# Two products of batch 1 moved between batch 0's tiles of scores, one value step put ahead of the fourth burst, and two kinds of setup matmuls cut into four

## The chip, the cores and the metric

The kernel runs on one core of a Trainium2 chip. The metric is the time of one execution on the device in microseconds (us), as the median of several runs; lower is better. The engines of the core are TensorE (PE in the profile, its weight loads PEld), VectorE (DVE), ScalarE (ACT), GpSimd (POOL) and SyncE (SP), which here only issues DMAs.

## The reference

A graph attention layer over 16 batches of 512 nodes with 512 features. A node may attend to the first 20 nodes only (the "keys"), in two directions d, with 16 heads of 32 features. The code is cut to what matters, with sizes for some symbols.

```python
row_zero = exp_v.sum(-1) == 0
q_exp = jnp.where(row_zero[..., None], 0.0, q[:, None, :])
self_feat = concatenate([exp_v, q_exp], axis=-1) @ W_self.T + b_self
output = self_feat
for d in range(2):
    A = adj_f if d == 0 else jnp.swapaxes(adj_f, 1, 2)
    A = A[:, :, :20, :]
    cond, vb = A.sum(-1), A @ w_bias + b_bias
    kv = self_feat[:, :20]
    qh = (self_feat @ Wq[d].T + bq[d]).reshape(B, N, 16, 32)
    kh = (kv @ Wk[d].T + bk[d]).reshape(B, 20, 16, 32)
    aff = einsum('bnhd,bmhd->bnhm', qh, kh) / sqrt(32)
    aff = where(cond[:, :, None, :] > 0, aff, NEG) + vb[:, :, None, :]
    w = softmax(aff, axis=-1)
    out_t = einsum('bnhm,bmf->bnhf', w, kv)
    output = output + einsum('bnhf,hgf->bnhg', out_t, Wout[d]) + bout[d]
return exp_v + relu(output)
```

## The kernel before

All matrices are float32. The kernel folds the query weights into the keys (so that scores are products of `self_feat` with a prepared matrix `g` per batch) and the output weights into the values. It has a setup and then a loop over the 16 batches.

**Order.** The order of instructions on every engine is the order in which the program text issues them (`manual_schedule`); waits between engines follow from the data. Tiles come from pools with few buffers, and a new tile in a buffer waits for the last use of the old one. In the loop the matmul banks of products and attention are four fixed ones (`bank(name, 0)` to `bank(name, 3)`, tag `acc0` to `acc3`); scores use pairs of banks from `ps_s`, two pairs in turn.

**The forms of a matmul.** Most matmuls are cut into four along their outputs: `for a in range(HL)` with R = 32 outputs each, so that four of them write the four quarters of a bank's partitions. In the profile such a group has the shape "128\*32", an uncut one "128\*128". Each float32 matmul shows as two records of PE and two of PEld.

**Setup** (lines 458 to 786). `kv_terms` (line 537) multiplies the first 20 nodes of all batches (`xkv`, 320 columns) with the self weights `ws_v`, in four steps k of the contraction and four banks fc; between steps stand the projection of the query condition (`ps_q`, lines 548 and 560) and the sum over `rsk` (line 555), which flags rows that are zero. `key_rows` (line 589) makes the projected keys `khD`, with VectorE copying them out of the bank (line 602). Then come 20 "bursts" (`keys`, line 672): each makes a part of `g`, with matmuls of the shape "32\*128", read by ScalarE (line 696) and VectorE (line 698). Between bursts PE does other work, so that the banks of a burst can be read: the rest of the key rows for the first four, and then what the list `plan` (line 726) names per burst, one letter per step:

- `v` and `w`: `values` (line 645), four (or eight) matmuls of the values with 512 columns; the fourth step of a tile copies it out on VectorE (line 660) and sends it off by DMAs issued on GpSimd (line 664). One `v` step stands ahead of the burst itself where n is 4 (line 749).
- `n`: `row_flags` (line 211), one matmul of a matrix of ones with the row sums, which gives the zero-row flags of batch 0 or 1.
- `p`: one of the seven products of batch 0 (below), with the VectorE step that reads it.
- `m`, `b`, `c`: bias terms.

Burst n in the program counts from 0; the text counts from one, so that the fourth burst is n = 3.

**Products.** The self features of nodes 20 to 511 are made in the way of a fast 2x2 block multiplication, with seven products per batch (`product(b, n)`, line 250) of 16 matmuls each, 246 columns wide. Products 1, 6, 7 and 4 add in turn onto the same two banks `ps_a` (acc0 and acc1), product 2 has `ps_d` (acc2), products 5 and 3 share `ps_c` (acc3). VectorE reads the banks between them: `partial` (line 285, L289) reads `ps_a` after products 1, 6, 7 and 4, two instructions each time; `joined` (line 297, L299) adds `ps_d` or `ps_c`. So product 6 must not start before the `partial` that follows product 1 has read `ps_a`.

**The loop.** Each batch b has four tiles nt of 128 nodes. A tile's `scores` (line 349) are 64 matmuls; `weigh` (line 376) then adds the mask, takes the maximum and subtracts it on VectorE (L379, L383, L387), `expo` takes the exponential on ScalarE (L392), `normal` (L415 to L417) divides by the sum, `turn` (L424) transposes the weights, and `attend` (L435) multiplies them with the values of the batch, once per batch, in tile 2 of the batch after. The products of batch b + 1 run within batch b: 1 and 2 behind the scores of tile 2, 6 ahead of the scores of tile 3, 7 and 5 behind them; 4 and 3 run in the next batch's tile 0. `weigh` of tile 2 takes a function `between` that puts `partial(b + 1, 0, 0)` on VectorE between the maximum and the subtraction. The masks go through `mask_mul` (ScalarE, L317), `mask_sum` (VectorE, L328), `mask_spread` (ScalarE, L337) and `full_add` (GpSimd, L344).

Around the change the PE order of batch 0 is: scores of tiles 0, 1 and 2; products 1, 2 and 6 of batch 1; scores of tile 3; products 7, 5 and 4; then tile 0 of batch 1, product 3, tile 1, the attention of batch 0.

Of the kernel before, what the change touches and what calls it, by code (L numbers as in the profile page):

```python
# [13 lines left out]
P = 128  # L14
# [4 lines left out]
def gat_kernel(  # L19
# [20 lines left out]
    nc = tc.nc  # L40
    B, F, N = xT.shape
    NG, L = adj.shape[3], adj.shape[4]
    H, DH = 16, 32
    C = F // P
    HL = P // DH
    NT = N // P
    BM = B * NG
# [4 lines left out]
    R = P // HL  # L52
# [20 lines left out]
    ws_v = const.tile([P, C, F], F32, name="ws_v")  # L73
# [137 lines left out]
    def row_flags(b):  # L211
        ps = bank(f"ps_nz{b}")
        nc.tensor.matmul(ps[:, :N], ones, rss[b], start=True, stop=True)  # L213
        nzs[b] = load.tile([P, N], F32, tag="nz", name=f"nz{b}")
        nc.vector.tensor_scalar(nzs[b], ps[:, :N], 0.0, None, ALU.not_equal)
# [109 lines left out]
    def mask_sum(b, h):  # L325

        add = conds[b, h] = msk.tile([P, 2 * S], F32, tag="add", name=f"add{b}_{h}")
        done["masks"] = nc.vector.tensor_reduce(add, prods.pop((b, h)), AX.X, ALU.add)  # L328
        adds[b, h] = msk.tile([P, 2, HL, S], F32, tag="both", name=f"both{b}_{h}")
# [128 lines left out]
    with tc.tile_pool(name="setup", bufs=1) as sp, tc.tile_pool(name="ps_acc", bufs=4, space=PSUM) as acc["pool"]:  # L458
# [12 lines left out]
        ones = sp.tile([P, P], F32, name="ones")  # L471
# [6 lines left out]
        with tc.tile_pool(name="setup_k", bufs=1) as sk:  # L478
# [58 lines left out]
            def kv_terms(fc, k):  # L537
                nc.tensor.matmul(  # L538
                    kv_ps[fc][:, :BM], ws_v[:, k, bass.ts(fc, P)], xkv[:, k],
                    start=(k == 0), stop=(k == C - 1),  # L540
                )

# [80 lines left out]
        with tc.tile_pool(name="setup_g", bufs=4) as sg:  # L623
# [101 lines left out]
            }  # L725
            plan = "mmvv bvv vvc vvc vvn vvw vvw vw wn p p p p p p p".split()

# [17 lines left out]
            for n, runs in enumerate(bursts):  # L745
                for i in range(len(rest)):
                    if (i < 1 and n > 0) or any(fc == 0 and (d, hg) == rest[0] for fc, hg, d, _, _ in runs):
                        key_rows(*rest.pop(0))
                if n == 4:
                    values(*steps["v"].pop(0)[1])  # L750
# [44 lines left out]
    with tc.manual_schedule():  # L795
# [10 lines left out]
        for b in range(B):  # L806
# [7 lines left out]
            for nt in range(NT):  # L814
# [13 lines left out]
                if nt == 0:  # L828
                    if b == 0:
                        for g in range(2):  # L830
                            scores(b, nt, g, ps[g])
                        mask_sum(b, 1)
                    else:
# [48 lines left out]
                if nt == 1:  # L882
# [11 lines left out]
                    for g in range(2):  # L894
                        scores(b, nt, g, ps[g])
                    if last:
                        for c in (0, 1):
                            nc.scalar.activation(biased[:, c], sfs[b][:, c], AF.Identity, bias=bo[:, c : c + 1])
# [17 lines left out]
                if nt == 2:  # L916
# [27 lines left out]
                    if more:  # L944
                        product(b + 1, 1)
                        product(b + 1, 2)
                        new_self(b + 1)
# [69 lines left out]
        b = B - 1  # L1017
# [77 lines left out]
```

## Time and profile before

| what | value |
|---|---|
| time, three runs | 582.24, 582.80 and 580.28 us; median 582.24 us |
| the profiled execution | 581.09 us, its span (first to last instruction) 579.3 us |
| mean granted clock of TensorE | 0.998 |
| PE busy | 572.1 us |
| DVE, POOL, ACT busy | 492.8, 405.5, 393.8 us |
| DMA | 123.26 MB, mean 213 GB/s |
| scores, the costliest group (L365) | 8192 records, 277.4 us |
| products (L283) | 3584 records of six groups, 29.6 to 59.4 us each |

All durations come from that one profiled execution. Its span begins with the first instruction; the rest of its 581.09 us lies around the span. A row of the timeline gives the start, the duration, the engine, the line, the operation with its tiles, the shape of the operands and the number of records (x); in brackets stands the idle time of the engine before it and what ended it. "issue" there means that the engine waited for nothing that the profile shows. A row of the windows view gives for each stretch its length and then, for PE, PEld, DVE, ACT and POOL, the busy time and the records, and at last the granted clock of PE, the mean busy share of the DMA engines and the rate in GB/s.

### The profile page before, as it was taken

The numbers are of one execution on the slowest core, as the hardware profiler recorded it, in microseconds if no ns is written. First come the engines' busy times: TensorE is split into PE (matmuls) and PEld (weight loads), VectorE is DVE, ScalarE is ACT, GpSimd is POOL, SyncE is SP. The second block draws the span as 40 slices with busy tenths as digits, with TensorE's granted clock in tenths as the row PEclk, the third lists the DMA queues.
The fourth block names the chain that finished last, engine by engine and source line by source line (L and its number), as shares of the span: only waits on it lengthen the run. The fifth ranks groups of instructions, "written<-read, shape, count | busy, mean of one in ns | idle before, by whom it ended". The sixth has DMA issues, their size and how long they took to land.

```text
span 579.3 us, 30986 instructions
## 1 busy us (share of the span) xinstructions
PE 572.1 (99%) x13496; PEld 434.0 (75%) x13496; DVE 492.8 (85%) x790; ACT 393.8 (68%) x1162; POOL 405.5 (70%) x383
## 2 busy tenths in 40 slices
PE   9999999999999999999999999999999999999996
PEld 6544458888878787878778787887887878787873
DVE  0685676979898989898999999898989898989896
ACT  1234554587878777778786868687887877777571
POOL 2636977648686776858585867786858677786874
PEclk9999999999999999999999999999999999999999
DMA  8999998757776777778576767576666766664404
GB/s 287 386 405 311 335 363 290 210 144 220 210 233 183 207 203 201 215 178 235 169 217 168 219 168 209 165 216 179 203 197 188 202 195 182 194 202 111 146 19 147
DMA packets 98787, 123.26 MB, mean 213 GB/s; under 512 B 18876, under 2 KB 66968, under 8 KB 96604
## 3 DMA queue, kind: packets, MB, share of 16 engines
q1 hardware_dynamic: 96124, 117.80, 66.2%
q0 software_dynamic: 1392, 2.43, 1.8%
q8 instruction: 106, 1.74, 1.3%
q10 hardware_dynamic: 1136, 1.06, 0.5%
q14 instruction: 29, 0.24, 0.1%
HBM read 82.30 MB, written 40.24 MB: 212 GB/s over the span
## 4 chain that ended last, share of the span: by engine, by line
PE 97%; DMA 1%; DVE 0%; issue 0%; SPq 0%; DVEq 0%
PE ps_s L365 46%; PE ps_a L283 19%; PE ps_c L283 9%; PE ps_o L435 6%; PE ps_d L283 5%; PE ps_v L654 3%; PE ps_k L596 3%; DMA ws_q<-in_wsT 1%; PE ps_o L798 1%; PE ps_kv L538 0%; PE ps_nz L213 0%; PE ps_s L354 0%; PE _g(0, 2, 0, 14, 16)0_440 L681 0%; PE _g(2, 2, 0, 14, 16)0_836 L681 0%; PE _g(1, 2, 0, 14, 16)0_644 L681 0%
## 5 line engine op out<-in xcount | busy, mean ns | idle before, releaser
L365 PEld LDWEIGHTS ps_s<-g,sf 128*32 128x32 f32 x8192 | 263.1, 110 | 21.8 <-issue 14.7
L365 PE MATMUL ps_s<-g,sf 128*32 128x152 f32 x8192 | 277.4, 293 | 0.7 <-issue 0.7
L337 ACT COPY both<-add 32x80 f32<-32x80 f32 x512 | 130.9, 256 | 61.0 <-DVE add L328 55.1
L417 POOL TENSOR_TENSOR s<-s,sm 128x640 f32<-128x640 f32 x63 | 80.4, 1276 | 96.0 <-DVE sm L416 73.5
L344 POOL TENSOR_TENSOR full<-cq,both 128x640 f32<-128x640 f32 x64 | 100.4, 1569 | 26.8 <-issue 20.9
L317 ACT ACTIVATE prod<-adj,wb_sb 128x80 f32<-128x80 int32 x330 | 112.4, 431 | 0.0
L392 ACT ACTIVATE s<-s 128x640 f32<-128x640 f32 x63 | 46.5, 738 | 55.4 <-DVE s L387 55.0
L449 POOL TENSOR_TENSOR o<-o,x 128x512 f32<-128x512 f32 x60 | 76.3, 1293 | 0.0
L379 DVE TENSOR_TENSOR full<-ps_s,full 128x608 f32<-128x608 f32 x63 | 48.7, 773 | 21.6 <-PE ps_s L365 19.0
L415 DVE TENSOR_REDUCE sm<-s 128x32 f32<-128x640 f32 x63 | 50.8, 806 | 10.7 <-ACT s L392 10.5
L283 PE MATMUL ps_a<-t,ws_s 128*32 128x246 f32 x1024 | 59.4, 371 | 0.0
L383 DVE TENSOR_REDUCE ps_s<-full 128x32 f32<-128x640 f32 x63 | 52.2, 828 | 2.2
L424 DVE STREAM_TRANSPOSE wt<-s 128x640 f32<-128x640 f32 x63 | 52.7, 837 | 0.6 <-POOL s L417 0.6
L387 DVE TENSOR_TENSOR s<-full,ps_s 128x640 f32<-128x640 f32 x63 | 51.5, 817 | 1.1
L289 DVE SCALAR_TENSOR_TENSOR sf<-nz,qw,ps_a 128x246 f32<-128x246 f32 x128 | 51.5, 442 | 0.2
L283 PEld LDWEIGHTS ps_a<-t,ws_s 128*32 128x32 f32 x1024 | 34.2, 110 | 16.7 <-issue 0.6
L328 DVE TENSOR_REDUCE add<-prod 128x80 f32<-128x960 f32 x32 | 36.8, 1149 | 7.2 <-ACT prod L317 7.2
L446 ACT ACTIVATE o<-o,bo 128x512 f32<-128x512 f32 x60 | 38.3, 710 | 0.6 <-DVE o L444 0.6
L248 POOL TENSOR_TENSOR t<-x,t 128x492 f32<-128x492 f32 x32 | 36.8, 1151 | 1.3
L248 POOL TENSOR_TENSOR t<-x 128x492 f32<-128x492 f32 x32 | 36.9, 1154 | 0.0
L435 PE MATMUL ps_o<-wt,vd 32*32 32x512 f32 (+5 forms) x816 | 36.8, 578 | 0.1
L444 DVE TENSOR_TENSOR o<-ps_o,sf 128x512 f32<-128x512 f32 x60 | 36.7, 668 | 0.0
(225 smaller groups left out, 715.4 us busy)
## 6 DMA issues: line engine op xcount, KB each, us to landing
g<-g_d SPq DMA_DIRECT2D x60, 304.0 KB
g_d<-st SPq DMA_DIRECT2D x16, 1064.0 KB
out_T<-o SPq DMA_DIRECT2D x60, 256.0 KB
xn<-in_xn SPq DMA_DIRECT2D x56, 256.0 KB
x<-in_xT SPq DMA_DIRECT2D x56, 256.0 KB
adj<-in_adj SPq DMA_DIRECT2D x60, 220.0 KB
nz<-nz_d SPq DMA_DIRECT2D x14, 256.0 KB
wk<-in_wkT SPq DMA_DIRECT2D x2, 1024.0 KB
```

The source lines that it names most:

```text
L248: done["xsum"] = nc.gpsimd.tensor_sub(t, one, two)
L283: nc.tensor.matmul(to, lhs, x[:, k], start=start, stop=stop, skip_group_check=n != 2)
L289: done["partial"] = nc.vector.scalar_tensor_tensor(to[:, i], nzs[b][:, half(l)], qw[:, 2 * f + i, b : b + 1], parts[b, "a"][i][:, :HN], AL ...
L317: nc.scalar.activation(p[:, :, l], a[:, :, l], AF.Identity, scale=wb_sb[:, l : l + 1])
L337: done["spread"] = nc.scalar.copy(adds[b, h][bass.ts(a, R), :, g], add[r].rearrange("p (t m) -> p t m", t=2))
L344: done["full"] = nc.gpsimd.tensor_add(f, cqs[b].unsqueeze(1).to_broadcast(shape), adds[b, nt // 2][:, nt % 2].unsqueeze(2).to_broadcast(sh ...
L365: nc.tensor.matmul(to, sfs[b][:, k, bass.ds(nt * P + (2 * g + j) * R, R)], of, start=(onto is None and k == 0 and (whole or j == 0)), stop ...
L383: nc.vector.tensor_reduce(mx, f, AX.X, ALU.max)
L417: done["normal"] = nc.gpsimd.tensor_mul(s, s, sm.unsqueeze(3).to_broadcast(full))
L424: nc.vector.transpose(wts[b][:, nt], s.rearrange("p a h m -> p (a h m)"))
L435: nc.tensor.matmul(banks[a][bass.ds(at // 2 * DH, n * DH)].rearrange("p (t n) -> p t n", n=32), vd[r, bass.ds(at * DH, n * DH)], wt[r, :, ...
L449: nc.gpsimd.tensor_add(o[:, c], o[:, c], xs[b][:, c])
```

## The change

- Products 1 and 2 of batch 1 no longer stand behind batch 0's third tile of scores (nt = 2): product 1 stands behind its first tile, product 2 behind its second. Other batches are as before. VectorE's order in the loop is the same; the `partial` that follows product 1 stays inside `weigh` of tile 2.
- One value step stands ahead of burst n = 3 as well as n = 4. As the number of steps is fixed, the seventh entry of `plan` (behind burst n = 10) has one `v` fewer. Three copies of value tiles on VectorE (L660) thereby come ahead of the evacuation of the next burst, and their DMAs on GpSimd's queue move with them.
- `row_flags` and `kv_terms` are cut into four matmuls of 32 outputs each, over the same columns.

```diff
     def row_flags(b):
         ps = bank(f"ps_nz{b}")
-        nc.tensor.matmul(ps[:, :N], ones, rss[b], start=True, stop=True)
+        for a in range(HL):
+            nc.tensor.matmul(ps[bass.ts(a, R), :N], ones[:, :R], rss[b], start=True, stop=True)
...
             def kv_terms(fc, k):
-                nc.tensor.matmul(
-                    kv_ps[fc][:, :BM], ws_v[:, k, bass.ts(fc, P)], xkv[:, k],
-                    start=(k == 0), stop=(k == C - 1),
-                )
+                for a in range(HL):
+                    nc.tensor.matmul(
+                        kv_ps[fc][bass.ts(a, R), :BM], ws_v[:, k, bass.ds(fc * P + a * R, R)], xkv[:, k],
+                        start=(k == 0), stop=(k == C - 1),
+                    )
...
-            plan = "mmvv bvv vvc vvc vvn vvw vvw vw wn p p p p p p p".split()
+            plan = "mmvv bvv vvc vvc vvn vvw vw vw wn p p p p p p p".split()
...
-                if n == 4:
+                if n in (3, 4):
                     values(*steps["v"].pop(0)[1])
                 keys(runs)
...
                     if b == 0:
                         for g in range(2):
                             scores(b, nt, g, ps[g])
+                        product(1, 1)
                         mask_sum(b, 1)
...
                     for g in range(2):
                         scores(b, nt, g, ps[g])
+                    if b == 0:
+                        product(1, 2)
...
                     if more:
-                        product(b + 1, 1)
-                        product(b + 1, 2)
+                        for n in (1, 2) if b > 0 else ():
+                            product(b + 1, n)
                         new_self(b + 1)
```

## The prediction

> **What bounds the kernel now.** I read the busy shares first, then the chain that ended last, and then the windows view of the long middle.
>
> ```profile
> PE 572.1 (99%) x13496; PEld 434.0 (75%) x13496; DVE 492.8 (85%) x790; ACT 393.8 (68%) x1162; POOL 405.5 (70%) x383
> ...
> PE 97%; DMA 1%; DVE 0%; issue 0%; SPq 0%; DVEq 0%
> ```
>
> ```profile
> 131.07:560.00 428.93, 428.93 (x11052) 341.83 (x11048) 392.49 (x607) 329.96 (x992) 312.75 (x269) 1.00 0.66 190
> ```
>
> TensorE is the bound: 97% of the chain is PE, and from 131.07 us on PE is busy in all of 428.93 us. So whatever delays or advances PE before 131 us reaches the end undiminished, and nothing is earned after it. All of the change lies in the setup (to 90 us) or in batch 0's tiles. That start is therefore the only stretch that matters. It is shown by PE's timeline: start, duration, engine, line, tiles, records, and in brackets the idle time before.
>
> ```profile
> 90.48 8.04 PE L365 MATMUL ps_s<-g,sf 128*32 128x152 f32 x241
> 98.67 4.34 PE L365 MATMUL ps_s<-g,sf 128*32 128x152 f32 x128 [0.15 <-issue]
> 103.59 0.59 PE L365 MATMUL ps_s<-g,sf 128*32 128x152 f32 x12 [0.59 <-issue]
> ```
>
> Three tiles of scores follow each other here, 128 records each. PE stops twice "for nothing that the profile shows", after record 241 and again 128 records later. No tile begins there (they begin at 128 and 256), so no semaphore of a tile is at work.
>
> ```profile
> q8 instruction: 106, 1.74, 1.3%
> ```
>
> The queue carries 106 packets, 1.74 MB. They are mainly for PE's 13496 matmul and 13496 weight-load records: 26992/106 = 255 per packet, that is 127 matmul records. The two stops are 128 records apart, so I read them as PE waiting for its next packet of instructions. What they cost comes from the rows after them.
>
> ```profile
> 104.14 1.84 PE L283 MATMUL ps_a<-x,ws_v 128*32 128x246 f32 x31
> 105.66 1.97 PE L283 MATMUL ps_d<-x,ws_v 128*32 128x246 f32 x32
> 107.32 1.97 PE L283 MATMUL ps_a<-t,ws_s 128*32 128x246 f32 x32
> 108.99 4.31 PE L365 MATMUL ps_s<-g,sf 128*32 128x152 f32 x125
> ```
>
> ```profile
> 123.90 4.44 PE L365 MATMUL ps_s<-g,sf 128*32 128x152 f32 x128
> 128.44 2.70 PE L435 MATMUL ps_o<-wt,vd 32*64 32x512 f32 x48
> 131.07 4.34 PE L365 MATMUL ps_s<-g,sf 128*32 128x152 f32 x128
> 135.23 1.84 PE L283 MATMUL ps_a<-x,ws_v 128*32 128x246 f32 x32
> ```
>
> An undisturbed tile takes 135.23 - 131.07 = 4.16 us, three take 12.48. Here they took 104.14 - 90.48 = 13.66, so the stops cost between 0.74 (the listed idle times) and 1.18 us. A product takes 107.32 - 105.66 = 1.66 us. The attention of batch 0 starts at 128.44, while its scores, 4.16 after 123.90, were over at 128.06: PE waits there too.
>
> **The change part by part.** *Products 1 and 2 of batch 1* (32 matmuls, no DMA, no copy) stood between the scores of tile 2 and product 6. They now stand behind tiles 0 and 1. Product 6 adds onto the banks that product 1 filled, so it must wait until VectorE has read them (L289, "partial"). On VectorE, whose order in the loop is unchanged, that read stands behind two operations on tile 2's scores:
>
> ```profile
> 104.44 0.79 DVE L379 TENSOR_TENSOR full<-ps_s,full 128x608 f32<-128x608 f32 x1 [0.42 <-PE ps_s L365]
> 105.27 0.83 DVE L383 TENSOR_REDUCE ps_s<-full 128x32 f32<-128x640 f32 x1
> 106.00 0.84 DVE L289 SCALAR_TENSOR_TENSOR sf<-nz,qw,ps_a 128x246 f32<-128x246 f32 x2
> ```
>
> So the first of the two reads ends 106.42 - 104.44 = 1.98 us after VectorE starts on tile 2. Before, the two products (3.32 us) covered that, and product 6 started at 107.32 without a wait. Now nothing stands between: with scores ending 0.30 us before L379 starts (104.44 - 104.14), PE idles about 2.3 us ahead of product 6. Everything on PE is queued behind it: product 6, tile 3's scores, products 7, 5 and 4.
>
> What the two products gain in their new places is the fetch stops. A packet that holds 32 product records and 96 of scores lasts 3.12 + 1.66 = 4.78 us instead of 4.16. From the first stop's end to the second's, 98.67 to 103.59, one packet needed 4.92 us, so a stop of some 0.1 us is left, once or twice. Bounds: 0 and 1.18; I take 0.2, near the first, since each packet but one holds a product's records.
>
> Now the start of VectorE's tile 2, which I call T (104.44 before): 90.48 for the first scores, plus 12.48, plus 3.32 for the two products now ahead of it, plus 0.2, plus 0.30, is 106.78, less what the setup gains (below, 0.57): 106.21, that is 1.77 us later. It decides what follows, because from T on no engine in the chain rests:
>
> ```profile
> 104.44:112.71 8.27, 8.27 (x208) 7.68 (x204) 8.20 (x13) 2.87 (x8) 6.08 (x6) 1.00 0.85 251
> 112.79:123.92 11.13, 11.13 (x276) 10.33 (x272) 7.26 (x12) 10.93 (x36) 6.53 (x8) 1.00 0.60 160
> ```
>
> ```profile
> 111.56 1.15 DVE L328 TENSOR_REDUCE add<-prod 128x80 f32<-128x960 f32 x1
> ```
>
> ```profile
> 128.27 0.63 DVE L299 TENSOR_TENSOR sf<-ps_c,sf 128x492 f32<-128x492 f32 x1
> ```
>
> In the first window VectorE (the third engine) works 8.20 of 8.27 us, up to the mask sum of L328. In the second ScalarE (the fourth) works 10.93 of 11.13: spread of the mask, exponential, row sums, mask products. Then VectorE again, to the joined block at 128.27 + 0.63 = 128.90, on which the attention's fourth bank waits. From product 6 on, PE has five products and three tiles of scores before it is there: 5 x 1.66 + 3 x 4.16 = 20.78 us from T + 1.98, so it arrives at T + 22.8, VectorE at T + 24.5. VectorE's chain decides, before and after, so the attention, and with it the end, moves by T's 1.77 us. PE's own wait of 2.3 us and that shift are one cost, not two.
>
> *The clock.* PE's granted clock (third number from the end) is 1.00 in all windows above, but none of them holds an idle time like the new one. PE is slow once in this trace, at the start:
>
> ```profile
> 4.19 5.73 PE L538 MATMUL ps_kv<-xkv,ws_v 128*128 128x320 f32 x16
> ```
>
> Eight matmuls took 5.73 us here; four of the same kind later take 2.39 (quoted below), so about 5.73 - 4.78 = 0.95 us went to that slow stage. If 2.3 us of idleness brought it back, the same price would fall due: the last rival. [...]
>
> *The value step* (four 128x512 matmuls) ahead of the fourth burst of keys. No work is added: the eleventh burst has one step fewer behind it.
>
> ```profile
> 35.58 0.30 PE L681 MATMUL _g(0, 2, 0, 14, 16)0_440<-khD,wq_sb 32*128 32x38 f32 x2
> ...
> 37.02 2.25 PE L596 MATMUL ps_k<-kvD,wk 128*32 128x304 f32 x32
> ...
> 52.74 0.30 PE L681 MATMUL _g(1, 2, 0, 14, 16)0_644<-khD,wq_sb 32*128 32x38 f32 x2
> ...
> 53.91 1.92 PE L654 MATMUL ps_v<-wo_sb,kvT 128*32 128x512 f32 x16
> 55.77 1.13 PE L213 MATMUL ps_nz<-rx,ones 128*128 128x512 f32 x2
> 56.82 0.41 PE L681 MATMUL s_g(1, 3, 0, 7, 16)0_683<-khD,wq_sb 32*128 32x171 f32 x2
> ```
>
> The fourth burst took 37.02 - 35.58 = 1.44 us, its like five bursts later 53.91 - 52.74 = 1.17: 0.27 us lost on keys that VectorE had not yet written. A step ahead of it covers that, as one does for the fifth burst. Gain 0.27; bounds 0 and 0.27. Three copies of values on VectorE, and their DMAs on POOL's queue, come a step earlier, ahead of two evacuations; PE has 1.86 us of steps between bursts there, so I cost that at nothing, and at one such copy (0.63 by L299, which reads a bank of nearly that size) if the cover failed.
>
> *The flags* (L213, twice): 56.82 - 55.77 = 1.05 us for a 128-output matmul among 32-output value steps.
>
> ```profile
> 57.84 2.78 PE L654 MATMUL ps_v<-wo_sb,kvT 128*32 128x512 f32 x24
> ...
> 60.55 0.52 PE L681 MATMUL s_g(2, 0, 0, 0, 16)0_721<-khD,wq_sb 32*128 32x304 f32 x2
> ```
>
> Twelve value matmuls take 2.71 us, eight 1.86: four more cost 0.85, and four 32-output flags have the same size and follow a value step. Gain 0.20 each, 0.40 together; bounds 0 and 0.40.
>
> *The input sums* (L538, "kv"): 16 matmuls become 64.
>
> ```profile
> 10.22 1.05 PE L548 MATMUL ps_q<-ws_q,q_sb 128*16 128x512 f32 x8 [0.30 <-DMA ws_q<-in_wsT]
> ```
>
> ```profile
> 11.28 1.91 PEld L538 LDWEIGHTS ps_kv<-xkv,ws_v 128*128 128x128 f32 x8 [0.93 <-DMA xkv<-in_xkvT]
> 11.31 2.39 PE L538 MATMUL ps_kv<-xkv,ws_v 128*128 128x320 f32 x8
> ```
>
> ```profile
> 17.48 8.39 PE L596 MATMUL ps_k<-kvD,wk 128*32 128x304 f32 x128 [0.20 <-DVE kvD L581]
> ```
>
> The first half is hidden: PE waits for ws_q at 10.22 and for the third piece of x at 11.28 whatever it did before. Key rows in the 32-output form take 8.39 us for 64 matmuls (128 records) at 304 columns; sixteen at 320 columns would take 8.39 / 64 x 16 x 320 / 304 = 2.21 us, against 2.39 for four 128-output ones, of which the last one's tail overlaps what follows. That is hardly a gain, and PE then waits for VectorE at 17.48 anyway. From the flags' rows a change between 32 and 128 outputs costs about 0.1 us (1.05 - 0.85 for two), and one more of them (before the sum over rsk, L555) lies on the path to 17.48. I take a loss of 0.1; bounds -0.1 and 0.4 (four changes). [...]
>
> Setup: 0.27 + 0.40 - 0.10 = 0.57 us gained. **Sum:** 1.77 us lost. The profiled execution took 581.09 us, so its like would take 582.9. That execution is 1.15 under the median of the three runs (582.24), from which I forecast 584.0.
>
> **The rivals.**
> *Product 6 finds its banks read* (faster). If L289 could run before tile 2's scores are through, the wait would not exist, and the kernel would gain the stops and the setup: 1.0 + 0.57, 580.7 us. It decides where L289 ends before T. For it: product 1 is done a tile earlier. Against it: VectorE's order keeps L289 behind L379, which waited for PE 0.42 us before.
> *The attention waits for something else* (no change). If PE's wait of 128.90 - 128.06 = 0.84 us around 128.44 hung on work at a fixed time, a landing of values for instance, PE's own account alone would count up to there: 2.3 of wait, less 0.98 of stops (1.18 - 0.2) and 0.57 of setup, is 0.75 us late, and that slack takes it up: 582.2. Against it: the windows show the chain without rest.
> *The stops stay* (slower). If packets stay late, T moves by 1.0 more: 585.0. For it: DMA share is 0.85 in that stretch.
> *The clock falls* in the new wait: 0.95 us more, 585.0. For it: the wait is the longest that PE would have in the loop. Against it: no row of this trace shows the clock falling after a wait.
>
> **How the numbers follow.** Forecast (+1.0 to +2.6) 0.62; product 6 without a wait 0.06; taken up by the attention 0.13; stops stay 0.13; clock 0.06. The three runs of before lie 2.5 us apart, so I add 1 us on either side: 581.2 to 585.8. About 0.5% (2.9 us) is what a measurement can tell from no change. Slower than 585.1: half of the clock's case, half of the stops', a tenth of the forecast's, 0.03 + 0.06 + 0.06, and 0.02 for scatter: 0.17. Faster than 579.3 is out of reach of every case but by scatter, 0.03. Same, 0.80.
>
> **What would show it.** The two issue stops in batch 0's scores gone or under 0.3 us; a new wait of PE at L284 (product 6) on VectorE's partial, 2.0 to 2.5 us; the attention 1.8 us later; the fourth burst at 1.17 us; flags without 128-output matmuls, the first scores at 89.9. No wait at product 6, or an attention that does not move with it, would prove me wrong.

## The result, and the profile after

The changed kernel takes 585.75 us (median of 5 runs, 585.48 to 586.05) against 581.79 us for the kernel before in the same comparison: ratio 1.0063, 95% interval 1.0042 to 1.0085. It is slower by 3.7 us by the ratio (4.0 by the medians), where 1.8 was forecast. The profiled execution took 585.50 us with a span of 583.3.

The busy shares and the chain that ended last, from the page of the changed kernel:

```profile
PE 572.6 (98%) x13604; PEld 431.7 (74%) x13604; DVE 493.2 (85%) x790; ACT 393.9 (68%) x1162; POOL 404.4 (69%) x383
...
PE 94%; DMA 3%; DVE 1%; POOL 0%; issue 0%; SPq 0%; ACT 0%; DVEq 0%; POOLq 0%
```

PE's busy time grew by 0.5 us only, the span by 4.0: the loss is waiting. PE's share of the chain fell from 97 to 94%, and VectorE and DMA took what it lost. PE's timeline around batch 0's tiles (start, duration, engine, line, tiles, shape, records, idle time before):

```profile
91.50 4.32 PE L366 MATMUL ps_s<-g,sf 128*32 128x152 f32 x128
95.63 1.84 PE L284 MATMUL ps_a<-x,ws_v 128*32 128x246 f32 x32
97.29 4.32 PE L366 MATMUL ps_s<-g,sf 128*32 128x152 f32 x128
101.42 1.84 PE L284 MATMUL ps_d<-x,ws_v 128*32 128x246 f32 x32
103.08 4.32 PE L366 MATMUL ps_s<-g,sf 128*32 128x152 f32 x128
109.66 1.87 PE L284 MATMUL ps_a<-t,ws_s 128*32 128x246 f32 x32 [2.26 <-POOL full L345]
...
115.46 1.88 PE L284 MATMUL ps_a<-t,ws_s 128*32 128x246 f32 x32
...
131.56 2.70 PE L436 MATMUL ps_o<-wt,vd 32*64 32x512 f32 x48 [0.87 <-PE ps_s L366]
```

The two stops within the scores are gone: each tile takes 4.13 us, and a product behind it 1.66. Product 6 (109.66) now waits 2.26 us. The row names GpSimd's L345 as what ended the wait, but the last thing that product 6 needs is VectorE's read of its banks, and VectorE's timeline has that read just ahead of it:

```profile
107.54 0.79 DVE L380 TENSOR_TENSOR full<-ps_s,full 128x608 f32<-128x608 f32 x1 [1.29 <-PE ps_s L366]
109.10 0.84 DVE L290 SCALAR_TENSOR_TENSOR sf<-nz,qw,ps_a 128x246 f32<-128x246 f32 x2
...
131.38 0.63 DVE L300 TENSOR_TENSOR sf<-ps_c,sf 128x492 f32<-128x492 f32 x1
```

T, VectorE's start on tile 2, is 107.54 instead of 104.44: 3.10 us later. The attention starts 3.12 later (131.56 for 128.44), so the shift of T passes through whole. The rows of the setup that are new in PE's timeline:

```profile
17.18 0.72 PE L598 MATMUL ps_k<-kvD,wk 128*32 128x304 f32 x8 [0.20 <-PE ps_kv L540]
18.58 7.88 PE L598 MATMUL ps_k<-kvD,wk 128*32 128x304 f32 x120 [0.68 <-DMA wk<-in_wkT]
```

```profile
74.53 1.87 PE L284 MATMUL ps_d<-x,ws_v 128*32 128x246 f32 x32
...
77.71 0.32 PE L683 MATMUL s_g(3, 0, 0, 0, 16)0_981<-khD,wq_sb 32*128 32x190 f32 x1 [0.29 <-issue]
...
78.23 1.87 PE L284 MATMUL ps_a<-t,ws_s 128*32 128x246 f32 x32
```

PE waits for the second piece of the key weights, and it stops for nothing that the profile shows in the burst between products 2 and 6 of batch 0: from one to the other it took 3.70 us (74.53 to 78.23), and 2.84 before (74.37 to 77.21), so 0.86 were lost. The stretches of the span, before and after, in us:

| stretch | before | after | difference |
|---|---|---|---|
| span's start to first key row | 17.48 | 17.18 | -0.30 |
| first key row to first scores | 73.00 | 74.32 | +1.32 |
| first scores to T | 13.96 | 16.04 | +2.08 |
| T to the attention | 24.00 | 24.02 | +0.02 |
| attention to the last matmul's start | 445.85 | 446.07 | +0.22 |
| last matmul's start to the end | 5.02 | 5.67 | +0.65 |

The setup was forecast to gain 0.57 and lost 1.02; the move was forecast at 2.34 and cost 2.08. The first row of the table says little about the edits: the first key row stands between 17.18 and 18.55 us in the profiles of this study, with PE's wait for `ws_q` between nothing and 1.7 us.

### The profile page after: what moved, and what is told of

The parts are those of the page before. It is cut to its first block, busy times and chain, and to the rows that moved or that the text cites. A ratio compares the mean times of both kernels' runs of the same rounds, so it can differ in the third digit from the quotient of the medians.

```text
span 583.3 us, 31203 instructions
## 1 busy us (share of the span) xinstructions
PE 572.6 (98%) x13604; PEld 431.7 (74%) x13604; DVE 493.2 (85%) x790; ACT 393.9 (68%) x1162; POOL 404.4 (69%) x383
## 4 chain that ended last, share of the span: by engine, by line
PE 94%; DMA 3%; DVE 1%; POOL 0%; issue 0%; SPq 0%; ACT 0%; DVEq 0%; POOLq 0%
PE ps_s L366 45%; PE ps_a L284 18%; PE ps_c L284 9%; PE ps_o L436 6%; PE ps_d L284 4%; PE ps_v L656 3%; PE ps_k L598 3%; DMA wk<-in_wkT 2%; DMA ws_q<-in_wsT 1%; PE ps_o L800 1%; PE ps_nz L214 0%; POOL full L345 0%; PE ps_s L355 0%; PE s_g(3, 0, 0, 0, 16)0_981 L683 0%; POOL s L418 0%
## 5 line engine op out<-in xcount | busy, mean ns | idle before, releaser
L345 POOL TENSOR_TENSOR full<-cq,both 128x640 f32<-128x640 f32 x64 | 100.2, 1566 | 26.7 <-issue 20.7
```

The costliest lines, as they stand in the source:

```text
L345: done["full"] = nc.gpsimd.tensor_add(f, cqs[b].unsqueeze(1).to_broadcast(shape), adds[b, nt // 2][:, nt % 2].unsqueeze(2).to_broadcast(sh ...
```

## The experiments

All kernels were timed beside the kernel before, whose medians in the four measurements were 582.64, 583.19, 582.89 and 582.80 us. The table has each one's ratio to it, what its profiled execution took above its own median, and the three stretches that its profile shows. Without stops the third is 16.04 us with both products ahead of T (three executions have it to 0.01) and 13.38 without them (the value step's execution, in which PE does not stop within these tiles and VectorE, without idle time, is itself not ready sooner).

| kernel | ratio, 95% interval | profiled less median | first key row to scores | scores to T | T to attention |
|---|---|---|---|---|---|
| move alone | 1.0041, 1.0027 to 1.0055 | +2.11 | 73.67 | 17.07 | 24.00 |
| sums alone | 1.0013, 1.0003 to 1.0023 | +1.01 | 73.00 | 14.81 | 23.95 |
| flags alone | 0.9992, 0.9982 to 1.0001 | +0.12 | 72.60 | 13.89 | 24.01 |
| value step alone | 0.9987, 0.9976 to 0.9998 | -0.31 | 72.97 | 13.38 | 24.20 |
| changed kernel again | 1.0059, 1.0046 to 1.0072 | -0.05 | 72.59 | 17.56 | 24.66 |
| changed, sums uncut | 1.0019, 1.0009 to 1.0030 | -0.23 | 72.58 | 16.62 | 24.66 |
| move, early read | 1.0028, 1.0015 to 1.0041 | -0.43 | 73.00 | 16.05 | 23.37 |
| all of these, row sums later | 1.0015, 1.0003 to 1.0027 | +0.51 | 72.60 | 17.45 | 23.47 |
| changed, other warm-up | 1.0045, 1.0025 to 1.0065 | -1.49 | 72.59 | 16.04 | 24.01 |
| flags, row sums last | 1.0029, 1.0015 to 1.0042 | -0.70 | 72.60 | 14.68 | 23.92 |
| move, early read, flags, row sums last | 1.0067, 1.0048 to 1.0086 | -1.63 | 72.60 | 16.35 | 22.46 |
| flags and value step | 0.9974, 0.9961 to 0.9987 | +2.06 | 72.59 | 16.05 | 24.19 |

### Each edit alone

The move alone:

```diff
+                        product(1, 1)
                         mask_sum(b, 1)
...
+                    if b == 0:
+                        product(1, 2)
...
-                        product(b + 1, 1)
-                        product(b + 1, 2)
+                        for n in (1, 2) if b > 0 else ():
+                            product(b + 1, n)
```

> Only the two products are moved; sums, flags and value step are as before. Theory A (VectorE's chain from tile 2 on sets the attention of batch 0, and the fetch stops end): scores start near 90.5 us; no stop over 0.2 us inside the three tiles; VectorE starts tile 2 2.1 us later (3.32 of products less 1.2 of stops); a wait of 2.0 to 2.5 us at product 6; the time 2.1 us above before. Rival B (the wait at product 6 is the whole cost and the attention's own wait absorbs some of it): the wait is there, but the time rises by 0.7 to 1.3 us. Rival C (the loss in the changed kernel's setup comes from the move as well, by another layout of instructions or tiles): scores start 0.8 us or more later than 90.5 and the time rises by 3 us or more.

584.75 us against 582.64: ratio 1.0041, 2.4 us (2.1 by the medians), near the 2.34 that the prediction's sum gives the move alone. Its profiled execution was 2.11 above its median and shows why single executions scatter (PE's timeline):

```profile
91.84 4.04 PE L365 MATMUL ps_s<-g,sf 128*32 128x152 f32 x114
96.48 0.59 PE L365 MATMUL ps_s<-g,sf 128*32 128x152 f32 x11 [0.60 <-issue]
...
111.04 1.87 PE L283 MATMUL ps_a<-t,ws_s 128*32 128x246 f32 x32 [2.25 <-POOL full L344]
```

The wait at product 6 is there (2.25). A stop stands after record 114 of the first tile, 127 records ahead of the stop after record 241 in the kernel before. With another one in the setup (73.67 instead of 73.00) and 1.03 us over the 16.04 up to T, this execution lost 1.7 us to stops. Rival C's sign is there too, scores that start late (91.84), but it isn't the move's doing: 0.69 of it lies before the first key row, where PE waits 1.7 us for `ws_q`, and 0.67 is the stop in the setup; a later run with the same move ("move, early read") has 73.00 there.

The sums alone, cut into four:

```diff
-                nc.tensor.matmul(
-                    kv_ps[fc][:, :BM], ws_v[:, k, bass.ts(fc, P)], xkv[:, k],
...
+                for a in range(HL):
+                    nc.tensor.matmul(
+                        kv_ps[fc][bass.ts(a, R), :BM], ws_v[:, k, bass.ds(fc * P + a * R, R)], xkv[:, k],
```

> Only the input sums are cut into four (48 more matmuls, 192 more instructions on TensorE before the key rows). Theory A (more instructions bring the first instruction packet of 16 KB forward, onto a DMA engine that is then carrying the key weights): first packet near 14.4 us instead of 22.2, one sixteenth of the second key weights lands 1 us or more after the other fifteen, TensorE waits 0.5 to 0.9 us for it near 18 us, and the places of all later packets move by 96 of 128 records, so that stops of TensorE may turn up elsewhere; the time 0.6 to 1.6 us above before. Rival B (the late landing was chance): the key weights land together as before, and the time is within 0.3 us of before. Rival C (a change between 32 and 128 outputs is what costs): no wait for a DMA, 0.1 to 0.4 us above before.

583.42 us, ratio 1.0013: 0.8 us slower, with an interval of 0.2 to 1.3. The wait for the key weights, on which theory A put the cost, is not in this profile, so its time came true without its mechanism. The sums' own price can be read on PE's path from the third step of the sums to the first key row (PE's timeline of this kernel):

```profile
11.28 2.36 PE L539 MATMUL ps_kv<-xkv,ws_v 128*32 128x320 f32 x32
...
17.67 8.39 PE L597 MATMUL ps_k<-kvD,wk 128*32 128x304 f32 x128 [0.21 <-PE ps_kv L539]
```

This way takes 6.39 us where it took 17.48 - 11.31 = 6.17: 0.22 lost. From there to the first scores nothing changes (73.00). What differs besides is where PE stops:

```profile
90.67 5.01 PE L365 MATMUL ps_s<-g,sf 128*32 128x152 f32 x145
97.11 8.00 PE L365 MATMUL ps_s<-g,sf 128*32 128x152 f32 x236 [1.43 <-issue]
```

The stop came after record 145 instead of 241, that is 96 earlier, and 48 more matmuls are 96 records. So this stop kept to a count of records and was moved by an edit far ahead of it. Two things in the traces speak for the ends of packets. Counted from the program's first matmul record, 13 of the 17 stops that the profiles list, whatever the kernel, stand at three places: behind 1349 or 1350 records in eight of the fourteen profiles, behind 1222 or 1223 in three, behind 1477 in two. And all 17 end 1.2 to 1.6 us after a packet of the instruction queue (q8; 1.74 MB in 106 packets in the kernel before, 16 KB each) has landed: here the packet landed at 95.52 and PE went on at 97.11, in the kernel before at 97.33 and 101.99 for 98.67 and 103.59.

The flags alone, cut into four (the diff is that of the change):

> Only the two flag matmuls are cut into four. Both theories of the setup: 0.20 us less for each, 0.40 us less in all by the timeline (scores start near 90.1 us); the time 0.4 us under before, hard to tell from no change. Theory A adds that 24 more instructions move the packets by 12 records only, so the stops in batch 0's scores stay where they were, near records 229 and 357. Rival: the gain is lost to a later wait and scores start at 90.5.

582.10 us, ratio 0.9992: 0.5 us faster, with no change still within the interval. In the profile the gain is exact: 72.60 from first key row to first scores instead of 73.00, 0.20 at each of the two. Six more matmuls are 12 records, and the stops stand 12 earlier:

```profile
91.15 7.66 PE L366 MATMUL ps_s<-g,sf 128*32 128x152 f32 x229
99.06 4.34 PE L366 MATMUL ps_s<-g,sf 128*32 128x152 f32 x128 [0.25 <-issue]
```

The value step ahead of the fourth burst alone (the diff is that of the change):

> Only the value step ahead of the fourth burst. Theory: the fourth burst takes 1.17 us instead of 1.44, scores start 0.27 us earlier, near 90.2; the time 0.3 us under before. Rival (the earlier copies of values on VectorE and their DMAs on GpSimd's queue delay later bursts): the fourth burst is shorter but scores start at 90.5 or later.

581.68 us, ratio 0.9987, 0.1 to 1.4 us faster. The profile does not show this as a gain of the setup: 72.97 against 73.00, as the rival said. The 0.27 at the fourth burst is there, and 0.25 is lost again at the seventh. VectorE's timeline around it, first of the kernel before, then of this one:

```profile
44.30 1.25 DVE L698 TENSOR_SCALAR st<-s_g(1, 0, 0, 0, 16)1_521 128x608 f32<-128x608 f32 x2 [0.53 <-POOL bo L621]
...
45.54 0.68 DVE L660 COPY v<-ps_v 128x512 f32<-128x512 f32 x1
```

```profile
44.80 0.68 DVE L660 COPY v<-ps_v 128x512 f32<-128x512 f32 x1
45.80 1.25 DVE L698 TENSOR_SCALAR st<-s_g(1, 0, 0, 0, 16)1_529 128x608 f32<-128x608 f32 x2 [0.32 <-issue]
```

The copy of the value tile (0.68) now stands ahead of the evacuation of the sixth burst instead of behind it, and the seventh burst's second bank comes free that much later. What the medians gain beyond the setup is not explained: its profiled execution had no stop within the tiles (13.38 from scores to T, against 13.96), but that is one execution.

By the ratios the four parts sum to 2.4 + 0.8 - 0.5 - 0.8 = 1.9 us. The whole costs 3.7.

### The changed kernel again, and without the cut sums

The changed kernel, with no edit:

> The changed kernel once more, to see which of its waits recur. Theory A (the extra instructions of the input sums bring the first packet of PE instructions to about 14.4 us, among the loads of the key weights, and put a packet's end into the bursts): about 585.5 us, 3.0 to 4.0 over the kernel before; the profile shows PE waiting 0.4 to 0.9 us for wk near 18 us, and the scores' third tile starts on VectorE about 16.0 us after the first scores. Rival (both were accidents of one execution): no wait for wk and no stop in the bursts in this profile, which then is over 1 us shorter than the first one's span of 583.3.

586.44 us, ratio 1.0059: the cost is the same, and theory A's waits in the setup are not. This profile has no wait for the key weights and no stop in the bursts, and its setup is the 0.41 shorter that the flags give. So both were accidents of one execution, which lost 1.73 us by them (74.32 less 72.59). But the rival is wrong as well, for the time did not fall. The loss lies elsewhere here (PE's timeline, then two windows: length, PE, PEld, DVE, ACT and POOL busy, granted clock, DMA share, GB/s):

```profile
94.56 0.58 PE L284 MATMUL ps_a<-x,ws_v 128*32 128x246 f32 x5
96.03 1.64 PE L284 MATMUL ps_a<-x,ws_v 128*32 128x246 f32 x26 [0.89 <-issue]
...
110.11 2.83 PE L284 MATMUL ps_a<-t,ws_s 128*32 128x246 f32 x32 [2.23 <-POOL full L345]
112.64 5.16 PE L366 MATMUL ps_s<-g,sf 128*32 128x152 f32 x128
117.58 1.88 PE L284 MATMUL ps_a<-t,ws_s 128*32 128x246 f32 x32
```

```profile
107.45:110.86 3.41, 1.18 (x27) 0.74 (x21) 2.84 (x5) 1.76 (x6) 2.16 (x2) 1.00 0.75 216
110.86:114.28 3.42, 3.42 (x52) 2.75 (x47) 3.39 (x6) 0.74 (x1) 1.29 (x2) 0.50 0.40 116
```

The stop stands after record 133 of the order (128 of scores, 5 of product 1): 241 less 108, and the change adds 54 matmuls. And after the wait at product 6 the granted clock is 0.50 for 3.41 us: product 6 and tile 3's scores take 7.47 us (110.11 to 117.58) where they took 5.80 in the first profile (109.66 to 115.46). Of these 1.67 us, 0.64 reach the attention (24.66 from T instead of 24.02); PE's idle time ahead of it, 0.87 in the first profile, is gone.

The changed kernel with `kv_terms` as before:

> The changed kernel with the input sums uncut (move, flags and value step remain). Theory A: first packet of PE instructions back at about 22 us, no wait for wk, first scores 72.5 to 72.7 us after the first key row if no packet stops PE in the bursts (73.0 before); time 584.0 to 584.6, that is the move's 2.1 to 2.4 less the flags' 0.4. Rival (the sums cost what they cost alone, 0.8 at most, or nothing beside the move): 585.2 to 585.8. A stop for a packet, if any, falls at record 101 or 102 of the first tile of scores (241 - 128 - 12).

584.43 us, ratio 1.0019, 1.1 us over the kernel before. That is the parts' sum without the sums (2.4 - 0.5 - 0.8 = 1.1): these three add up. The changed kernel of the same measurement is 2.3 us slower by the ratios (1.0059 less 1.0019), and the intervals do not overlap. So the sums, expected at 0.1, cost 0.8 alone and some 2.3 beside the other edits. The profile shows the stop after record 229 (128 of scores, 32 of product 1, 69 of scores), 241 less 12, and not at 102, where I had put it: PE did not stop there. It also shows the low clock again:

```profile
98.60 2.13 PE L366 MATMUL ps_s<-g,sf 128*32 128x152 f32 x58 [0.17 <-issue]
...
108.88 3.38 PE L284 MATMUL ps_a<-t,ws_s 128*32 128x246 f32 x32 [2.23 <-POOL full L345]
...
116.35 1.87 PE L284 MATMUL ps_a<-t,ws_s 128*32 128x246 f32 x32
```

Every run lists the mean granted clock of each execution. Of the 37 executions of kernels with the 2.2 us wait at product 6, 14 lie at 0.996 or less. Of the 163 of all others, the kernel before among them, none does. The clock's record in the traces allows a reading of why it falls in some only. There the stretches at full speed are whole numbers of times 3.413 us long (102.40, 105.81 and 467.63 us are 30, 31 and 137 times; 570.03 in the kernel before and 573.44 in the first profile of the changed one are 167 and 168 times), and each fall after the wait lasts 3.41. From these lengths I take it, as an estimate, that the clock changed at steps of 3.41 us. The place of the steps differs: the first change stands between 4.4 and 7.0 us (6.62 in the kernel before), while PE starts at 1.04 in each profile. Where the clock fell, one such step held the whole wait, with PE busy in 1.18 us of it: 107.45 to 110.86 here, 105.66 to 109.07 in the kernel with the sums uncut. In the three other profiles with the wait a step ends within it (at 109.41, 110.22 and 107.52), and PE is busy for 1.40 us or more in each of their steps. A wait of 2.24 us at a random place lies whole in a step in (3.41 - 2.24) / 3.41 = 34% of cases, an estimate from these lengths; 14 of 37 are 38%. Two falls in five profiles are too few to show that this is the cause.

### Where the time of the move comes from

The move alone, with VectorE's first read of `ps_a` put into tile 1:

```diff
                     if b == 0:
                         product(1, 2)
+                        new_self(1)
...
-                    s = weigh(b, nt, pair)
+                    s = weigh(b, nt, pair, (lambda: partial(1, 0, 0)) if b == 0 else None)
...
-                        new_self(b + 1)
-                    s = weigh(b, nt, pair, (lambda: partial(b + 1, 0, 0)) if more else None)
+                        if b > 0:
+                            new_self(b + 1)
+                    s = weigh(b, nt, pair, (lambda: partial(b + 1, 0, 0)) if more and b > 0 else None)
```

> The move alone, but VectorE reads product 1's banks within tile 1 instead of tile 2 (the copy of the first twenty nodes on ScalarE goes with it), so product 6 has nothing to wait for. Theory A (VectorE's and ScalarE's chain from tile 2 on sets the attention): PE's 2.3 us ahead of product 6 vanish, and nearly as much of it comes back ahead of the attention (2.0 to 2.5 us there instead of 0.85); only the two reads, 0.76 us, are gone from the chain: attention 23.2 to 23.4 us after VectorE's start on tile 2 (24.0 in all runs so far), time 0.5 to 1.0 under the move alone, about 584.0. Rival (the wait at product 6 is the cost): attention wait stays 0.85, time 582.4. Second rival (the attention hangs on something at a fixed time): 584.75, as the move alone.

Ratio 1.0028, 0.8 us under that of the move alone, though in another measurement and with intervals that overlap. PE's timeline:

```profile
106.69 1.87 PE L283 MATMUL ps_a<-t,ws_s 128*32 128x246 f32 x32
...
113.36 1.87 PE L283 MATMUL ps_a<-t,ws_s 128*32 128x246 f32 x32 [0.67 <-DVE sf L289]
...
121.36 2.39 PE L365 MATMUL ps_s<-g,sf 128*32 128x152 f32 x64 [0.69 <-DVE sf L289]
...
130.39 2.70 PE L435 MATMUL ps_o<-wt,vd 32*64 32x512 f32 x48 [0.84 <-PE ps_s L365]
```

Product 6 waits for nothing, and 2.20 us of waiting stands at three later places, two of them new, each ended by VectorE (or, at the attention, by what the chain feeds it). I had expected it all ahead of the attention; its sum is right. The attention comes 23.37 us after T, 0.63 earlier than in the move alone; the two reads that left the stretch took 0.76. The rival's sign is there (0.84 ahead of the attention, as it was), but not its time: with the 2.25 us of product 6's wait gone and nothing in its place the kernel would be as fast as the one before, which the interval excludes. The wait at product 6 shows where VectorE's chain stands; it is not the cost by itself.

Then the chain's ScalarE part was shortened: early read, 32-output flags, and batch 2's four row sums (2.45 us ahead of batch 1's second mask products) put behind these products.

```diff
-                    if b == 0:
-                        for j in range(4):
-                            row_sum(2, j)
                     turn(*prev)
...
                         mask_mul(b, 1)
+                        if b == 1:
+                            for j in range(4):
+                                row_sum(2, j)
                         product(b, 4)
...
                         mask_count(b, 1)
+                        if b == 1:
+                            row_mask(b + 1)
```

> Move, early read as in the run before, 32-output flags, and batch 2's four row sums (2.45 us of ScalarE between tile 3's exponential and batch 1's second mask products) put behind those products. Theory A (that stretch of ScalarE is in the chain to the attention): attention wait under 0.5 us, time 2 to 3 under the early read alone, about 581.2, 1 us under the kernel before. Rival (the row sums are beside the chain): attention wait 2.0 or more, 583.6, the early read less the flags' 0.4.

Ratio 1.0015, 2 us slower than theory A said. The attention wait is not gone, it has another cause (PE's waits, then the issues of the values' loads on SP's queue in this kernel, and in the changed kernel):

```profile
PE ps_o L436 <- DMA vd<-bd_d: 0.9, 1, 0.9
...
L141 SPq DMA_DIRECT2D vd<-bd_d x4: 325/412/419, 127.9 to 129.2; - x4
```

```profile
L141 SPq DMA_DIRECT2D vd<-bd_d x4: 325/416/886, 125.0 to 126.8; - x4
```

The attentions stand at 131.50 and 131.56, but the loads are issued 2.9 us later. My edit caused it: the store of the row flags stands ahead of these loads on SP's queue, and it waits for GpSimd's flags, which wait for the row sums. So this run could not test the chain. Two more put the sums behind the mask spread of tile 0, and the flags and their store into tile 1:

```diff
                     mask_spread(b, 1, (2, 3))
+                    if b == 1:
+                        for j in range(4):
+                            row_sum(2, j)
...
+                    if b == 1:
+                        row_mask(2)
                     if b > 0 and more:
                         load_nz(b + 1, done["weigh"])
```

First with the flags and the kernel before, then with move, early read and flags:

> The kernel before with 32-output flags, and batch 2's row sums moved on ScalarE from tile 3 of batch 0 to behind the mask spread of batch 1's tile 0 (the row flags on GpSimd and their store on SP's queue go to tile 1, so that they don't stand ahead of the loads of the values). Theory A (that stretch of ScalarE sets the attention): attention less than 23.6 us after VectorE's start on tile 2 (24.0 before), PE without idle time ahead of it, 0.4 to 0.8 us from there and 0.4 from the flags: 0.8 to 1.2 under the kernel before. Rival (the attention hangs on the values' loads or on PE alone): the flags' 0.4 alone.

> Move, early read and 32-output flags as in the earlier run, with batch 2's row sums and flags put where the run e7_late has them. Theory A (in the earlier run SP's queue held the values' loads behind the store of the row flags, which waited for the sums): no wait for vd, attention wait under 0.5 us instead of 0.94, and 0.5 to 1.5 us faster than that run, so between 0.5 under and 0.5 over the kernel before. Rival (the values land at that time anyway): wait for vd stays, 0.7 to 1.1 over the kernel before.

In both, PE has no idle time ahead of the attention, which in the first comes 23.92 us after T, where PE itself is ready, and not under 23.6 as expected. In the time theory A is wrong for both. PE's timeline of the second:

```profile
128.82 2.24 PE L436 MATMUL ps_o<-wt,vd 32*64 32x512 f32 x48
...
139.95 1.87 PE L284 MATMUL ps_a<-t,ws_s 128*32 128x246 f32 x32 [1.29 <-DVE sf L290]
...
154.41 2.40 PE L366 MATMUL ps_s<-g,sf 128*32 128x152 f32 x64 [1.40 <-DVE sf L290]
...
162.53 2.24 PE L436 MATMUL ps_o<-wt,vd 32*64 32x512 f32 x48
```

The attention comes 22.46 after T instead of 23.37: the row sums were in the chain. But the next one comes 162.53 - 128.82 = 33.71 us later instead of 31.05 (33.26 in the run without the move). The 2.45 us of ScalarE now delay batch 1's tiles, VectorE is late again there, and PE waits 1.29 and 1.40 us ahead of the products and scores of batch 2. The ratios, 1.0029 and 1.0067, are losses. The work that was moved within this stretch moved the wait.

### Packets and the sums

The changed kernel with 15 more, smaller warm-up matmuls, by which the packets should end 30 records earlier:

```diff
-            for _ in range(7):
+            for _ in range(2):
                 nc.tensor.matmul(warm[:, :P], ones, ones, start=True, stop=True)
+            for n in range(20):
+                nc.tensor.matmul(warm[bass.ts(n % HL, R), :P], ones[:, :R], ones, start=True, stop=True)
```

> The changed kernel with other warm-up matmuls: 2 of 128 outputs and 20 of 32 outputs instead of 7 of 128, that is 15 more, so 30 more records of PE ahead of everything; what is computed stays. Ends of packets then fall 30 records earlier: at record 103 of the first tile of scores instead of 133 from the first scores (product 1's fifth). Theory A (the sums cost by where they put the packets' ends, and one packet less falls among the key weights): near the kernel with the sums uncut, 1.2 to 2.0 over the kernel before. Rival (the sums cost the same wherever the packets end): 3.3 to 3.8 over the kernel before, as the changed kernel.

Ratio 1.0045 with an interval of 1.0025 to 1.0065: between the two forecasts, and it excludes neither the sums' whole cost nor most of theory A. The profiled execution had no stop at all up to T (16.04) and was the second fastest of its kernel, 1.49 under the median. That the packets' ends are what makes the sums dear is not shown by it.

It does give a size for what the edits cost without stops: its span of 581.6 us stands against 579.6 in the value step's execution, which had no stop up to T either. That is 2.0 us of the 3.7. The rest would then lie in what the changed kernel loses more often or more heavily to stops, a late load or the low clock: its two profiles lost 1.73 in the setup, and 1.52 to a stop and 0.64 to the clock; the kernel before lost 0.58 up to T in its one profile. This is an estimate from five executions, too few to show it.

### The two edits that cost nothing alone

The kernel before with the flags and the value step, without move and cut sums:

> The kernel before with the two edits that cost nothing alone: 32-output flags and the value step ahead of the fourth burst; no move, no cut sums. By the traces of the single edits (flags 0.40 us less in the setup; the value step 0.27 won at the fourth burst and 0.25 lost at the seventh, net nothing): 0.4 under the kernel before, first scores 72.5 to 72.7 us after the first key row (73.0 before). Rival, by the medians of the two single runs (0.5 and 0.75 under, if both are real and add up): 1.2 under. In either case faster than the changed kernel by over 3.5.

581.08 us against 582.80, ratio 0.9974 (0.9961 to 0.9987): 0.8 to 2.3 us faster than the kernel before, and the fastest of all. The setup is 0.41 shorter, which is the traced gain; the medians of the single runs added up to 1.2, and it is nearer that. The interval excludes the traced 0.4, so most of this gain has no cause that the traces show. The profiled execution happens to be the slowest of its six, and shows the largest stop of this study:

```profile
89.95 3.54 PE L366 MATMUL ps_s<-g,sf 128*32 128x152 f32 x102
95.60 4.33 PE L366 MATMUL ps_s<-g,sf 128*32 128x152 f32 x127 [2.12 <-issue]
100.25 5.47 PE L366 MATMUL ps_s<-g,sf 128*32 128x152 f32 x154 [0.31 <-issue]
```

PE stops after record 102 (229 less 127) and again 127 records on. T comes 16.05 us after the first scores instead of 13.38, 2.7 us that are stops, and the execution was 2.06 over the median.

## Why the prediction was right and wrong

The direction and the wait were foreseen; the size was not. The measured 585.75 us lies in the stated 581.2 to 585.8 by 0.05 us, with a change twice the forecast 1.8. That it lies inside is luck: a cost that the sum did not have used up the upper margin. (The lower end, 581.2, is a microsecond below what its rule gives, 582.24 + 1.0 - 1 = 582.24; the upper end follows from it.)

**The direction and the mechanism of the move: right.** Stops gone in the profile of the changed kernel (forecast 0.2 left, none measured), a new wait at product 6 (2.3 forecast, 2.26), its cause VectorE's read behind two operations on tile 2's scores, and the attention moving with T. T to the attention is 24.00, 24.02, 24.00, 23.95 and 24.01 in five kernels whose T lies between 104.44 and 108.91, so no work at a fixed time takes the shift up. The term of 2.34 for the move is 2.08 in the profiles and 2.4 (1.6 to 3.2) as a ratio.

**The input sums: the step that failed.** "I take a loss of 0.1; bounds -0.1 and 0.4." Measured are 0.8 alone and about 2.3 beside the other edits. The step counted the matmuls' own time and changes of form, and these were near: 0.22 on PE's path to the first key row, within the bounds. It left out that 48 more matmuls move the stops by 96 records. The prediction had read the stops as waits for packets, and then used that for the scores alone. That they move by just that is shown (241 to 145, 229 and 133). That this is what the sums cost beyond 0.22 is not shown: the run with other warm-up matmuls left it open, the stops' size differs from execution to execution, and why the sums cost more beside the other edits than alone stays open.

**The value step: half wrong.** 0.27 was won where forecast. The cover of the three copies, which I cost at nothing, failed at the seventh burst: 0.25 there, below the 0.63 that I had put on one copy. The edit's net gain in the setup is nothing. The single run and the one with the flags were 0.8 and 1.5 us faster, where the traces explain 0 and 0.4; this stays open.

**The flags: right.** 0.40 forecast, 0.40 in every profile that has them.

**"Nothing is earned after 131 us": right for gains, not for scatter.** From the attention to the last matmul's start the profiles lie between 445.7 and 447.4 where no row sum was moved, and from there to the end between 4.94 and 5.84, without relation to the edits. The 0.65 us that the changed kernel lost at the very end belong to this.

**The rivals.** Product 6 with its banks read: wrong, it waited. The attention taking the shift up: wrong. Stops that stay: gone in two of five profiles with the wait, 0.6 to 1.5 us up to T in the other three, so this case was live in single executions. (The share of 0.85 that the prediction gave for it belongs to 104.44 to 112.71 us; in the stretch of the stops, 90.48 to 104.00, the DMA share was 0.72.) The clock falling in the new wait: forecast as the least likely, at 0.95 us. It happened in 2 of those 5 profiles and, by the mean clock, in 14 of 37 executions; the price on PE is 1.67, of which 0.64 reach the attention, on average 0.24 by an estimate (14 of 37).

**The size.** Of 3.1 us in T, the forecast had 1.77. The setup of that profile was 1.59 worse than forecast and the move 0.26 better. The second profile of the same kernel has a setup 0.41 shorter than before and loses as much to a stop and the clock instead. So the first profile's wait for the key weights cost that execution, but the slowdown does not need it, though I read it as the cause at first.

## What to carry to other kernels

PE stopped here for up to 2.1 us at one place and went on 1.2 to 1.6 us after a packet of instructions had landed; 48 more matmuls moved such stops by 96 records. So an edit that multiplies small instructions may have a second price beside their time (here 0.22 us in the rows, 0.8 to 2.3 in the runs, the difference not explained): weigh its own run and not only its rows. Products moved ahead of another engine's critical operation set it back here (3.32 us of them put T 2.66 later between executions without stops), and the wait that stood on TensorE for it was the sign of it, not the cost: removing it moved 2.20 us of it to later places. When single edits are at stake by half a microsecond, time each alone: here two of four carried a gain, 0.26% together, that the other two hid. And one profile is one execution: the 1.7 us that the first one lost in its setup were gone in the second, and the time was the same.

## What the runs showed that was not expected

- PE stopped 13 of 17 times at the same three counts of matmul records from the program's start, and always went on 1.2 to 1.6 us after a packet of 16 KB of the instruction queue had landed, for 0 to 2.1 us at one place, and differently in the two profiled executions of the changed kernel. The executions of the move alone and of the two kept edits that lost 1.7 and 2.7 us to stops were 2.1 us over their medians, and one with none, of the changed kernel with another warm-up, was 1.5 under; but with the flags and the row sums last, four listed stops of 2.0 us stood in an execution 0.7 under its median.
- After an idle time of 2.2 us the granted clock was 0.50 for 3.41 us in two of the five profiles with such a wait, and product 6 with the scores behind it took 7.47 us instead of 5.80, the same in both profiles that caught it.
- 2.45 us taken from ScalarE's part of the chain brought the attention forward by 0.9 us (22.46 from T instead of 23.37) and set the next one back by 2.7.
- From the second batch on, a batch of the loop lasts 30.47 or 30.48 us from attention to attention, but in ten of the fourteen profiles one to three single batches are 0.1 to 0.6 us longer, at other places each time. This is scatter that no edit here explains.
